# Seven-block left products in a fourth gated step, and layernorms moved between ScalarE and VectorE

## The chip, the core and the metric

The kernel runs on one core of a Trainium2 chip. The engines named here are TensorE (PE, with its weight loads as PEld), VectorE (DVE), ScalarE (ACT), GpSimd (POOL) and SyncE (SP), which issues nearly all transfers. The metric is the device time of one execution in microseconds. The kernel before took 1408.14 us, the median of 3 runs from 1408.05 to 1408.65.

## The reference

The input x holds 64 graphs of 256 nodes with 128 features, in float32, and one adjacency matrix adj (256 x 256) is shared by all. Four graph layers follow each other, each wrapped as x = layernorm(x + layer(x)):

- layer 0: an attention layer with its own way of pairing nodes, a softmax, and a second weight for the node itself
- layer 1: attention with leaky ReLU scores, a softmax over the neighbours, the weighted sum, and an ELU
- layer 2: five gated steps. In each, m = adj @ h; then r, z = sigmoid of (m times a weight + h times a weight), hv = tanh(m times a weight + (r * h) times a weight), and h = (1 - z) * h + z * hv
- layer 3: x times a weight plus adj @ x, adj^2 @ x and adj^3 @ x times weights

The layernorm subtracts the mean over the features and divides by the standard deviation.

## The kernel before

**Units and lanes.** Two graphs make a unit, so there are 32 units, numbered 0 to 31. A unit's data is a tile of 128 partitions by 512 columns: two graphs times two chunks of 128 nodes, times 128 features. Ten lanes (`LANES`) of buffers let ten units be under way at once. Lane k works on units k, k + 10 and so on.

**The planner sets the order.** The kernel doesn't issue instructions as its loops run. `add` records each as a task with an engine, a planned duration, and the cells it reads and writes. `Plan.run` then goes through planned time. Whenever an engine is free it takes the ready task with the smallest key, and the order in which tasks are taken is the order of the program on each engine. The key (`first`) is the unit's number times `PERIOD` plus the task's due time. The due time grows along the unit's own chain of dependences, by the planned duration and a latency, times `PACE` (2.9), or times `PACE_GATED` (1.56) in layer 2. On the chip each engine executes its list in that fixed order, and a late operand holds up everything behind it on that engine. A product can only be planned when one of the 8 PSUM banks is free.

**The left product m = adj @ h in layer 2.** `layer2` has two ways to make it, chosen by `fast = step in FAST and far(u, step - 1)`.

- The plain way, `left` (L771): two products of 256 columns for each of the two graphs, four in all, into one bank. Then ACT copies the bank to m (L839).
- The fast way, `left_fast`: DVE forms sums and differences of the four blocks of h (L781, L783, L784). Seven products of 128 columns (L788) go into two banks x and y. ACT copies the first (L800), and DVE combines the rest into m (L815, L818, L820, L821). The combined blocks of adj lie in `adjTf`.

`far(u, step)` says whether the unit's h is turned by a DVE transpose and transfers through DRAM (the tile `hb`), rather than on PE. Units 0 and 1 start with that from step 2 (`FIRST_FAR`), and unit 31 stops it at step 1 (`LAST_FAR`). With `FAST = (2, 3, 4)` there are 91 fast steps and 69 plain ones.

After m is there, the products of 512 columns with the gate weights follow (L843): h and m for r, then, once ACT has the tanh for r and DVE has r * h, m for hv and z, and r * h with u5. The activations are L854, L862 and L871, and DVE's updates L857, L869, L873 and L875. The new h is transposed on DVE (L883, L896) and sent through `hb`.

**The layernorm.** `layernorm` takes statistics on DVE (L566, L568). POOL raises the variance to the power -1/2 (L571). The four pieces of 128 features are then normalised either on ACT (L584, which needs one more DVE instruction, L575, for the shift) or on DVE (L588, L592):

```
by_act = u >= TIGHT and plan.layer in NORM
```

With `TIGHT = 4` and `NORM = (0, 1, 2, 3)` ACT does it in all four layers from unit 4 on.

**The end.** The last three units (29 to 31) write their output in two transfers, one per chunk of nodes (L955), each after the two normalisations of its chunk. All others use a single one (L951).

Of the kernel before, what the change touches and what calls it, by code (L numbers as in the profile page):

```python
# [18 lines left out]
LEAD = 10  # L19
BANKS = 8  # L20
BL = 32
FAST = (2, 3, 4)
NORM = (0, 1, 2, 3)
SCALES = True
TIGHT = 4
FIRST_FAR = {0: 2, 1: 2}
# [1 line left out]
PERIOD = 43e3  # L28
TAIL = 0.3
LATE = 6  # L30
PACE = 2.9
PACE_GATED = 1.56
HOLD = 80
DIRECT_ROWS = 3
# [28 lines left out]
class Plan:  # L63
# [17 lines left out]
    def add(self, eng, ns, fn, reads=(), writes=(), after=(), wait=0, group=None, dma=False):  # L81
        t = Task(eng, ns, fn, self.unit, wait, dma or eng == "sp")
        for c in reads:
            t.deps.update(c.writers)
            c.readers.append(t)
        for c in writes:
            if c.bank and not c.writers:
                t.takes.append(c)
            if group is None or c.group is not group:
                c.waits = {w for o in (c, *c.over) for w in (*o.writers, *o.readers)} - {t}  # L90
                c.writers, c.readers, c.group = [], [], group
            t.deps.update(c.waits)
            if c.bank and c.writers:

                t.deps.add(c.writers[0])
            c.writers.append(t)
        t.deps.update(after)
        t.deps.discard(t)
        for c in {id(c): c for c in (*reads, *writes) if c.bank}.values():
            c.users += 1  # L100
            t.banks.append(c)
        t.step = self.step = self.step + 1
        t.layer = self.layer
        t.rank = self.rank
        self.tasks.append(t)
        return t
# [4 lines left out]
    def run(self, spawn, units, key):  # L111
# [22 lines left out]
        def start(lane):  # L134
            mine = [u for u in queue if u % LANES == lane]
            if mine:
# [5 lines left out]
                for t in self.tasks[seen:]:  # L142
                    t.due = max([d.due + (PACE_GATED if t.layer == 2 else PACE) * (d.ns + (
                        d.wait + self.LATENCY["sp" if d.dma else d.eng] if d.dma or d.eng != t.eng else self.OWN[t.eng]))
# [52 lines left out]
def kernel(  # L197
# [30 lines left out]
    NC = N // P  # L228
    UB = 2
    NU = B // UB  # L230
# [18 lines left out]
    def bank():  # L249
        return Cell(bank=True)  # L250
# [166 lines left out]
    for t, wT, n in ((wx0, woT, C0), (ws0, wselfT, D + 2)):  # L417
        ps = bank()
# [85 lines left out]
    def far(u, step):  # L504


        return step >= FIRST_FAR.get(u, -1) and step < LAST_FAR.get(NU - 1 - u, STEPS + 1)
# [8 lines left out]
    def turned(u, L, step):  # L516

        t = L["xT0"]  # L520
        if not far(u, step):
            feature_major(X[u], lambda g: X[u].ap[:, g // NC, g % NC, :], t)
            return t
        v = L["v"]
        add(DVE, 1050, lambda: nc.vector.transpose(  # L525
            v.ap.rearrange("p (a g i) -> p g a i", g=G, i=BL),
            X[u].ap.rearrange("p b c (j a) -> p (b c) a j", j=BL)), (X[u],), (v,))
        add("sp", 560, lambda: nc.sync.dma_start(L["hb"].ap, v.ap), (v,), (L["hb"],))
        parts = object()
        for q in range(P // BL):  # L530
            add("sp", 640, lambda q=q: nc.sync.dma_start(
                t.ap.rearrange("p (g q i) -> p g q i", g=G, i=BL)[:, :, q],
                L["hb"].ap[q * BL : (q + 1) * BL].rearrange("j (a g i) -> (j a) g i", g=G, i=BL)),
                (L["hb"],), (t,), group=parts)
        return t
# [20 lines left out]
                ps.ap[:, g * P : (g + 1) * P], view()[:, g : g + 1].to_broadcast([P, P]), ident.ap), (src, ident), (ps,))  # L556
        return ps, lambda: ps.ap.rearrange("q (b c p) -> q b c p", b=UB, c=NC)

    def layernorm(u, L, pairs, swap=False, centred=False):

        st, ve, rstd = L["st"], L["ve"], L["rstd"]
        sts, xs = object(), object()
        for k, (c, view) in enumerate(pairs):
            add(DVE, 330, lambda k=k, view=view: nc.vector.bn_stats(st.ap[:, k, :], view().rearrange("p j d -> p d j")),  # L566
                (c,), (st,), group=sts)
        add(DVE, 150, lambda: nc.vector.tensor_scalar(  # L568
            ve.ap.rearrange("p (k j) -> p k j", k=2), st.ap.rearrange("p k (j s) -> p k j s", j=2)[:, :, :, 2], 1.0 / D, EPS,
            op0=ALU.mult, op1=ALU.add), (st,), (ve,))  # L570
        add(POOL, 1050, lambda: nc.gpsimd.tensor_tensor(rstd.ap, ve.ap, nhalf.ap, op=ALU.pow), (ve, nhalf), (rstd,))  # L571
        by_act = u >= TIGHT and plan.layer in NORM

        if by_act and not centred:
            add(DVE, 120, lambda: nc.vector.scalar_tensor_tensor(  # L575
                ve.ap.rearrange("p (k j) -> p k j", k=2), st.ap.rearrange("p k (j s) -> p k j s", j=2)[:, :, :, 1], -1.0,
                rstd.ap.rearrange("p (k j) -> p k j", k=2), op0=ALU.mult, op1=ALU.mult), (st, rstd), (ve,))
        for k, (c, view) in enumerate(pairs):
            for j in range(2):
                b, ch = (j, k) if swap else (k, j)  # L580
                at = slice(2 * k + j, 2 * k + j + 1)
                shift, col = (ones, slice(0, 1)) if centred else (ve, at)
                if by_act:
                    add(ACT, 400, lambda j=j, b=b, ch=ch, view=view, at=at, shift=shift, col=col: nc.scalar.activation(  # L584
                        X[u].ap[:, b, ch, :], view()[:, j, :], AF.Identity, bias=shift.ap[:, col], scale=rstd.ap[:, at]),
                        (c, shift, rstd), (X[u],), group=xs)
                elif centred:
                    add(DVE, 260, lambda j=j, b=b, ch=ch, view=view, at=at: nc.vector.tensor_scalar(  # L588
                        X[u].ap[:, b, ch, :], view()[:, j, :], rstd.ap[:, at], 1.0, op0=ALU.mult, op1=ALU.add),
                        (c, rstd), (X[u],), group=xs)  # L590
                else:
                    add(DVE, 260, lambda k=k, j=j, b=b, ch=ch, view=view, at=at: nc.vector.tensor_scalar(  # L592
                        X[u].ap[:, b, ch, :], view()[:, j, :], st.ap[:, k, 3 * j + 1 : 3 * j + 2], rstd.ap[:, at],
                        op0=ALU.subtract, op1=ALU.mult), (c, st, rstd), (X[u],), group=xs)
# [172 lines left out]
    def left(ps, src, b, lhs=None, mat=adjT):  # L767

        lhs = lhs or (lambda b, mc: src.ap[:, b, mc, :])
        for mc in range(NC):  # L770
            add(PE, mm_ns(N), lambda b=b, mc=mc: nc.tensor.matmul(  # L771
                ps.ap[:, b * N : (b + 1) * N], lhs(b, mc), mat.ap[:, mc, :],
                start=(mc == 0), stop=(mc == NC - 1)), (src, mat), (ps,))
# [49 lines left out]
    def layer2(u, L):  # L823
        h, ht = turned(u, L, -1), X[u]
        for step in range(STEPS):
            m, at = L["m"], len(plan.tasks)
            fast = step in FAST and far(u, step - 1)
            ps_m = None if fast else bank()
# [94 lines left out]
    def layer3(u, L):  # L923
        xT = turned(u, L, STEPS)
        ps_a, aT, s = bank(), L["m"], L["z"]
        for b in range(UB):
            left(ps_a, X[u], b)
        add(ACT, 500, lambda: nc.scalar.copy(aT.ap, ps_a.ap), (ps_a,), (aT,))
        tail = list(ps_a.writers)

        ps = [bank() for _ in range(NC)]

        def view(c):
            return ps[c].ap.rearrange("p (k b d) -> p k b d", k=2, b=UB)

        for k, src in enumerate((xT, aT)):
            for c in range(NC):
                for b in range(UB):
                    add(PE, mm_ns(N), lambda k=k, src=src, c=c, b=b: nc.tensor.matmul(  # L939
                        view(c)[:, :, b, :], bn(src.ap)[:, b, c * P : (c + 1) * P], w3.ap[:, k],  # L940
                        start=(k == 0 and b == 0), stop=(k == 1), skip_group_check=True), (src, w3), (ps[c],), tail)
        for c in range(NC):
            add(ACT, 300, lambda c=c: nc.scalar.copy(s.ap[:, c * N : (c + 1) * N], ps[c].ap[:, N : 2 * N]), (ps[c],), (s,), group=ps)
        for c in range(NC):
            for mc in range(NC):
                add(PE, mm_ns(N), lambda c=c, mc=mc: nc.tensor.matmul(  # L946
                    ps[c].ap[:, 0:N], a2T.ap[:, mc, c * P : (c + 1) * P], s.ap[:, mc * N : (mc + 1) * N],
                    start=False, stop=(mc == NC - 1), skip_group_check=True), (a2T, s), (ps[c],))
        layernorm(u, L, [(ps[c], lambda c=c: view(c)[:, 0]) for c in range(NC)], swap=True)
        if u < NU - 3:  # L950
            add("sp", 450, lambda: nc.sync.dma_start(out_u[u], X[u].ap), (X[u],), ())  # L951
            return

        for c, done in enumerate((plan.tasks[-4:-2], plan.tasks[-2:])):
            add("sp", 450, lambda c=c: nc.sync.dma_start(out_u[u][:, :, c], X[u].ap[:, :, c]), (), (), done)  # L955
# [50 lines left out]
```

The softmax here doesn't subtract the row's maximum and nothing guards it: scores larger than these inputs give would overflow.

## Time and profile before

| | before |
|---|---|
| median of the runs | 1408.14 us |
| the profiled execution | 1408.72 us |
| its span, first to last instruction | 1406.5 us |
| PE busy | 1396.0 us (99%) |
| DVE busy | 1135.0 us (81%) |
| ACT busy | 939.2 us (67%) |
| POOL busy | 142.4 us (10%) |
| granted PE clock | 0.997 |

A busy time is the time in which at least one instruction of the engine ran. PE's instructions are pipelined and their ends are modelled, so its busy share says less than what it waited for and how far apart its instructions start. A float32 product shows as two instructions. In a group of instructions the columns are the number of them, busy time and mean ns of one, then the idle time of the engine just before them and what ended it. An engine's idle time only matters where it holds up the work that ends last.

### The profile page before, as it was taken

How to read it: one execution, taken by the hardware profiler on the slowest of the kernel's cores; microseconds unless marked ns; L12 is line 12 of the kernel's file. 1: busy time of each engine (PE TensorE's matmuls, PEld its weight loads, DVE VectorE, ACT ScalarE, POOL GpSimd, SP SyncE). 2: the span in 40 equal slices, each digit the busy share in tenths (PEclk: the TensorE clock that was granted, in tenths of full speed). 3: DMA queues.
4: the chain of work that ended last, by engine and by line, in shares of the span. 5: the costliest groups of instructions: out<-in, count | busy, mean ns of one | idle time of the engine just before them, and what ended most of it. 6: DMA issues, size and time to landing. Idle time of an engine off the chain costs nothing.

```text
span 1406.5 us, 20482 instructions
## 1 busy us (share of the span) xinstructions
PE 1396.0 (99%) x6163; PEld 961.8 (68%) x6163; DVE 1135.0 (81%) x2746; ACT 939.2 (67%) x2125; POOL 142.4 (10%) x134
## 2 busy tenths in 40 slices
PE   8999999999999999999999999999999999999998
PEld 8866666676666676676666677676666666666776
DVE  7988888879878788878788788888768888988642
ACT  5797647547766677757677778887766555566454
POOL 0110001001011001011000111021000000101011
PEclk9999999999999999999999999999999999999999
DMA  4213545454554445555445554545554443455411
GB/s 118 61 48 85 120 95 116 100 118 100 132 117 109 97 100 120 121 118 116 99 99 121 126 114 102 114 111 116 116 120 93 107 110 82 116 119 116 110 49 50
DMA packets 533246, 146.96 MB, mean 104 GB/s; under 512 B 460688, under 2 KB 498320, under 8 KB 533136
## 3 DMA queue, kind: packets, MB, share of 16 engines
q1 hardware_dynamic: 532336, 145.13, 46.6%
q8 instruction: 50, 0.82, 0.2%
q14 instruction: 60, 0.49, 0.1%
q10 hardware_dynamic: 800, 0.52, 0.1%
HBM read 81.10 MB, written 64.46 MB: 103 GB/s over the span
## 4 chain that ended last, share of the span: by engine, by line
PE 98%; DVE 1%; ACT 1%; DMA 0%; issue 0%; POOL 0%; SPq 0%; POOLq 0%; ACTq 0%; DVEq 0%
PE ps L843 48%; PE ps L771 12%; PE ps L788 10%; PE ps L939 8%; PE ps L695 4%; PE ps L725 4%; PE ps L946 4%; PE ps L690 2%; PE ps L619 2%; PE ps L738 2%; PE ps L344 0%; DMA m<-row 0%; PE ps L512 0%; PE ps L908 0%; ACT e L714 0%; PE ps L555 0%
## 5 line engine op out<-in xcount | busy, mean ns | idle before, releaser
L843 PE MATMUL ps<-m,gT 128*128 128x512 f32 x960 | 462.4, 593 | 0.4 <-DVE m L821 0.3
L571 POOL TENSOR_TENSOR rstd<-ve,nhalf 128x4 f32<-128x4 f32 x128 | 141.7, 1108 | 1258.9 <-DVE ve L568 1127.3
L843 PEld LDWEIGHTS ps<-m,gT 128*128 128x128 f32 x960 | 173.0, 190 | 124.9 <-issue 102.3
L862 ACT ACTIVATE e<-ps,bias 128x512 f32<-128x512 f32 x160 | 109.9, 688 | 119.4 <-PE ps L843 116.9
L854 ACT ACTIVATE e<-ps,bias 128x512 f32<-128x512 f32 x160 | 109.9, 688 | 84.8 <-PE ps L843 83.7
L843 PE MATMUL ps<-e,u5T 128*128 128x512 f32 x320 | 163.3, 592 | 0.0
L871 ACT ACTIVATE p<-ps,bias 128x512 f32<-128x512 f32 x160 | 109.7, 686 | 41.0 <-PE ps L843 38.5
L771 PE MATMUL ps<-adjT,x 128*128 128x256 f32 x512 | 135.1, 379 | 0.0
L873 DVE SCALAR_TENSOR_TENSOR p<-e,p 128x512 f32<-128x512 f32 x160 | 109.2, 683 | 23.7 <-ACT p L871 22.9
L788 PEld LDWEIGHTS ps<-adjTf,ht 128*128 128x128 f32 x546 | 88.0, 191 | 47.6 <-issue 38.4
L771 PEld LDWEIGHTS ps<-adjT,x 128*128 128x128 f32 x512 | 93.2, 190 | 35.2 <-issue 25.6
L788 PEld LDWEIGHTS ps<-adjTf,e 128*128 128x128 f32 x728 | 95.3, 192 | 15.0 <-issue 12.4
L788 PE MATMUL ps<-adjTf,e 128*128 128x128 f32 x728 | 102.9, 275 | 0.0
L843 PEld LDWEIGHTS ps<-e,u5T 128*128 128x128 f32 x320 | 59.8, 190 | 58.8 <-issue 45.0
L843 PE MATMUL ps<-xT,gT 128*128 128x512 f32 x192 | 97.8, 593 | 0.0
L788 PE MATMUL ps<-adjTf,ht 128*128 128x128 f32 x546 | 91.9, 274 | 0.0
L839 ACT COPY m<-ps 128x512 f32<-128x512 f32 x69 | 40.2, 583 | 70.6 <-PE ps L771 69.7
L857 DVE SCALAR_TENSOR_TENSOR e<-e,xT 128x512 f32<-128x512 f32 x96 | 65.7, 684 | 22.8 <-ACT e L854 22.1
L714 ACT ACTIVATE e<-m,esd 128x256 f32<-128x256 f32 x116 | 83.1, 763 | 0.9 <-DMA m<-row 0.9
L525 DVE STREAM_TRANSPOSE p<-x 128x512 f32<-128x512 f32 x61 | 67.1, 1100 | 15.1 <-ACT x L584 14.7
L695 PEld LDWEIGHTS ps<-ht,p 128*128 128x128 f32 x512 | 66.5, 190 | 12.1 <-issue 11.0
L566 DVE BATCH_NORM_STATS2 st<-ps 128x6 f32<-128x256 f32 x128 | 50.9, 421 | 25.2 <-PE ps L946 19.6
(174 smaller groups left out, 2640.4 us busy)
## 6 DMA issues: line engine op xcount, KB each, us to landing
hb<-p SPq DMA_DIRECT2D x182, 256.0 KB, 2.4
ht<-hb SPq DMA_DIRECT2D x484, 64.0 KB, 2.6
xT<-hb SPq DMA_DIRECT2D x244, 64.0 KB, 2.7
m<-row SPq DMA_DIRECT2D x58, 256.0 KB, 4.0
hb<-p SPq DMA_DIRECT2D x124, 64.0 KB, 1.8
ht<-hb SPq DMA_DIRECT2D x31, 256.0 KB, 3.2
out_dram<-x SPq DMA_DIRECT2D x29, 256.0 KB, 2.5
m<-in_x_dram SPq DMA_DIRECT2D x96, 64.0 KB, 2.7
```

Source lines behind the costliest of these rows:

```text
L525: add(DVE, 1050, lambda: nc.vector.transpose(v.ap.rearrange("p (a g i) -> p g a i", g=G, i=BL), X[u].ap.rearrange("p b c (j a) -> p (b c) ...
L571: add(POOL, 1050, lambda: nc.gpsimd.tensor_tensor(rstd.ap, ve.ap, nhalf.ap, op=ALU.pow), (ve, nhalf), (rstd,))
L695: add(PE, mm_ns(D + 2), lambda b=b, ic=ic, kc=kc, yv=yv: nc.tensor.matmul(yv()[:, ic, :], p.ap[:, b * NC + kc, ic * P : (ic + 1) * P], h.a ...
L714: add(ACT, 600, lambda g=g, b=b: nc.scalar.activation(e.ap[:, g, :].rearrange("p (c n) -> p c n", c=NC), ev()[:, b], AF.Prelu, bias=esd.ap ...
L771: add(PE, mm_ns(N), lambda b=b, mc=mc: nc.tensor.matmul(ps.ap[:, b * N : (b + 1) * N], lhs(b, mc), mat.ap[:, mc, :], start=(mc == 0), stop ...
L788: add(PE, mm_ns(P) + 4, lambda: nc.tensor.matmul(ps.ap[:, at * P : (at + 1) * P], lhs(), mat.ap[:, k, c * P : (c + 1) * P], start=True, st ...
L843: add(PE, mm_ns(T), lambda: nc.tensor.matmul(ps.ap, w(), rhs.ap, start=start, stop=stop, skip_group_check=True), (c, rhs), (ps,), after)
L854: add(ACT, 600, lambda ps_g=ps_g, up=up: nc.scalar.activation(r.ap, ps_g.ap, AF.Tanh, bias=bias2.ap[:, 1:2], scale=0.5 / up), (ps_g, bias2 ...
L862: add(ACT, 600, lambda ps_g=ps_g, up=up: nc.scalar.activation(z.ap, ps_g.ap, AF.Tanh, bias=bias2.ap[:, 0:1], scale=0.5 / up), (ps_g, bias2 ...
L871: add(ACT, 600, lambda ps_v=ps_v, up=up: nc.scalar.activation(v.ap, ps_v.ap, AF.Tanh, bias=bias2.ap[:, 2:3], scale=1 / up), (ps_v, bias2), ...
L873: add(DVE, 600, lambda: nc.vector.scalar_tensor_tensor(v.ap, z.ap, 1.0, v.ap, op0=ALU.add, op1=ALU.mult), (v, z), (v,))
L939: add(PE, mm_ns(N), lambda k=k, src=src, c=c, b=b: nc.tensor.matmul(view(c)[:, :, b, :], bn(src.ap)[:, b, c * P : (c + 1) * P], w3.ap[:, k ...
```

## The change

- `FAST` gains step 1, so step 1 of every unit that is `far` by then is made the fast way.
- `NORM` loses layer 1, so its four normalisations are on DVE in all units.
- `layernorm` gets the argument `last`. It is set in layer 3 for units 29 to 31, and there the first chunk is normalised on DVE and the second on ACT.
- `PACE` goes from 2.9 to 2.8, which changes the due times outside layer 2.

```diff
--- before.py
+++ after.py
@@ -19,8 +19,8 @@
 LEAD = 10
 BANKS = 8
 BL = 32
-FAST = (2, 3, 4)
-NORM = (0, 1, 2, 3)
+FAST = (1, 2, 3, 4)
+NORM = (0, 2, 3)
 SCALES = True
 TIGHT = 4
 FIRST_FAR = {0: 2, 1: 2}
@@ -28,7 +28,7 @@
 PERIOD = 43e3
 TAIL = 0.3
 LATE = 6
-PACE = 2.9
+PACE = 2.8
 PACE_GATED = 1.56
 HOLD = 80
 DIRECT_ROWS = 3
@@ -556,7 +556,7 @@
                 ps.ap[:, g * P : (g + 1) * P], view()[:, g : g + 1].to_broadcast([P, P]), ident.ap), (src, ident), (ps,))
         return ps, lambda: ps.ap.rearrange("q (b c p) -> q b c p", b=UB, c=NC)
 
-    def layernorm(u, L, pairs, swap=False, centred=False):
+    def layernorm(u, L, pairs, swap=False, centred=False, last=False):
 
 
 
@@ -576,11 +576,13 @@
                 ve.ap.rearrange("p (k j) -> p k j", k=2), st.ap.rearrange("p k (j s) -> p k j s", j=2)[:, :, :, 1], -1.0,
                 rstd.ap.rearrange("p (k j) -> p k j", k=2), op0=ALU.mult, op1=ALU.mult), (st, rstd), (ve,))
         for k, (c, view) in enumerate(pairs):
+
+            act = by_act and (k or not last)
             for j in range(2):
                 b, ch = (j, k) if swap else (k, j)
                 at = slice(2 * k + j, 2 * k + j + 1)
                 shift, col = (ones, slice(0, 1)) if centred else (ve, at)
-                if by_act:
+                if act:
                     add(ACT, 400, lambda j=j, b=b, ch=ch, view=view, at=at, shift=shift, col=col: nc.scalar.activation(
                         X[u].ap[:, b, ch, :], view()[:, j, :], AF.Identity, bias=shift.ap[:, col], scale=rstd.ap[:, at]),
                         (c, shift, rstd), (X[u],), group=xs)
@@ -946,7 +948,7 @@
                 add(PE, mm_ns(N), lambda c=c, mc=mc: nc.tensor.matmul(
                     ps[c].ap[:, 0:N], a2T.ap[:, mc, c * P : (c + 1) * P], s.ap[:, mc * N : (mc + 1) * N],
                     start=False, stop=(mc == NC - 1), skip_group_check=True), (a2T, s), (ps[c],))
-        layernorm(u, L, [(ps[c], lambda c=c: view(c)[:, 0]) for c in range(NC)], swap=True)
+        layernorm(u, L, [(ps[c], lambda c=c: view(c)[:, 0]) for c in range(NC)], swap=True, last=u >= NU - 3)
         if u < NU - 3:
             add("sp", 450, lambda: nc.sync.dma_start(out_u[u], X[u].ap), (X[u],), ())
             return
```

The lines after the inserted ones move by 2 in the changed kernel, so L788 is L790 there.

## The prediction

> **What bounds the kernel now.** I read the page's busy times first, then the chain that ended last, then what TensorE (PE) itself waited for, and only then the groups of instructions that the change touches. The page gives the span, the busy time of each engine and the chain by engine:
>
> ```profile
> span 1406.5 us, 20482 instructions
> PE 1396.0 (99%) x6163; PEld 961.8 (68%) x6163; DVE 1135.0 (81%) x2746; ACT 939.2 (67%) x2125; POOL 142.4 (10%) x134
> PE 98%; DVE 1%; ACT 1%; DMA 0%; issue 0%; POOL 0%; SPq 0%; POOLq 0%; ACTq 0%; DVEq 0%
> ```
>
> A modelled busy share of 99% alone would not settle it, but the chain is 98% PE, and the waits of PE (who was waited for, us in total, times, longest) are these three and no more:
>
> ```profile
> PE ps L725 <- DVE p L718: 2.3, 1, 2.3
> PE ps L344 <- POOL ident masks.py:199: 1.4, 1, 1.4
> PE ps L843 <- DVE m L821: 0.3, 1, 0.3
> ```
>
> The first two lie in the first 30 us. From there to about 1398 us PE is fed without a gap, so the time is PE's work plus a start and a tail. Less PE work shortens the kernel by just that amount, as long as VectorE (DVE) still keeps up. The table by stretches says how near DVE is to its own limit (start:end, length, then busy us of PE, PEld, DVE, ACT, POOL). The second row is a usual stretch and the first is the densest after the start-up:
>
> ```profile
> 315.00:350.00 35.00, 35.00 (x154) 22.83 (x153) 33.40 (x84) 26.35 (x62) 4.21 (x4) 1.00 0.45 101
> 595.00:630.00 35.00, 35.00 (x155) 24.48 (x154) 28.73 (x69) 19.83 (x46) 4.43 (x4) 1.00 0.45 99
> ```
>
> Even at 33.40 of 35 us PE did not wait. The prices come from the chain in order of time (start, us) for PE, and from the groups for the others:
>
> ```profile
> 608.16 0.89 PE ps L788 x8
> 610.35 1.73 PE ps L771 x8
> ...
> L781 DVE TENSOR_TENSOR e<-ht 128x256 f32<-128x256 f32 x91 | 37.6, 413 | 0.2 <-DMA ht<-hb 0.2
> L783 DVE TENSOR_TENSOR e<-e,ht 128x128 f32<-128x128 f32 x91 | 25.7, 283 | 0.6
> L784 DVE TENSOR_TENSOR e<-e,ht 128x128 f32<-128x128 f32 x91 | 25.9, 284 | 0.8
> L815 DVE TENSOR_TENSOR m<-ps,e 128x256 f32<-128x256 f32 x91 | 38.2, 420 | 30.6 <-PE ps L788 29.5 <-ACT e L714 0.2
> L839 ACT COPY m<-ps 128x512 f32<-128x512 f32 x69 | 40.2, 583 | 70.6 <-PE ps L771 69.7 <-DVE st L566 0.6 <-ACT e L714 0.2
> L584 ACT ACTIVATE x<-ht,ve,rstd 128x128 f32<-128x128 f32 x112 | 48.9, 485 | 20.4 <-DVE ve L575 20.4
> L592 DVE TENSOR_SCALAR x<-ht,st,rstd 128x128 f32<-128x128 f32 x16 | 4.6, 336 | 0.0
> ```
>
> Each float32 product is recorded as two instructions, so four 256-column products (x8) take 1.73 us and four 128-column ones 0.89 us.
>
> **What the Trainium skill says.** "TensorE: Matmul & The Clock Gate", section Back-to-back issue gap, gives N / 2.4 + 2.5 ns for a warm isolated matmul: 55.8 ns at 128 columns, 109 ns at 256. The trace has four times these per product (0.223 and 0.432 us), so it agrees in ratio: seven small products (28 x 55.8 = 1.56 us) are cheaper than four large ones (16 x 109 = 1.75 us). "VectorE: DVE Perf Modes", section The perf-mode tier table, says that a float32 tensor_scalar runs twice as fast as a tensor_tensor, but not from PSUM. Here L592 takes 336 ns from SBUF and 401 ns from PSUM. "ScalarE: Activation LUTs", section What ACT_TABLE_LOAD costs, prices an activation at 186 ns + 0.833 ns per element plus about 93 ns for each pointer operand. With two of them at 128 elements that is an estimate of 479 ns, against 485 measured.
>
> **The change part by part.** *Step 1 joins the fast steps.* A fast step needs its input by way of the transfer through hb, which units 2 to 31 have at step 1. Units 0 and 1 start that later. So 30 steps change, and fast steps go from 91 to 121. Each loses four L771 products, 4 x 0.4325 = 1.73 us, and gains seven L788 products. At 0.2225 each (0.89 / 4) these are 1.56; where the trace shows eight instructions in 0.90 us they are 1.575. The gain per step is 0.155 to 0.17 us, I take 0.163, and 30 steps give **4.9 us** of PE work (4.65 to 5.2).
>
> DVE gets seven instructions per step: 413 + 283 + 284 + 420 + 413 + 281 + 411 = 2505 ns, or 75.2 us for 30 steps. ACT loses the 583 ns copy L839 and gains the 266 ns copy L800, so 9.5 us less. I cost the DVE work at nothing, since PE's other work hides it. Without cover, a step's product on m would start later by 420 + 413 + 281 + 411 less the copy's 583 = 0.94 us. The cover can be read from the order in which the program's instructions stand on PE. Between the last block of a fast step and the first product that reads its m, the kernel before has at least 2.15 us of other PE work (median 3.9, seven steps at or under 2.2). The changed one has at least 2.19 (median 3.9, and the next shortest 2.6). The four combining instructions need about 1.5 us plus hand-offs, and with that cover 91 steps waited 0.3 us in all. A new step also holds two PSUM banks where it held one. No PE wait of today is for a bank, so that is 0 too.
>
> *Layer 1's normalisation goes to DVE.* Units 4 to 31 are concerned: 28 x 4 = 112 activations of 485 ns leave ACT (54.3 us), 112 tensor_scalars of 336 ns come to DVE (37.6 us), and 28 L575 of 153 ns leave it (4.3 us). Nothing of it is on PE. The unit's own path gets shorter.
>
> The sum for DVE is 1135.0 + 75.2 + 37.6 - 4.3 + 2.4 (the last units, below) = 1246 us of about 1401, or 89%. That is an upper end, because durations overlap: consecutive 512-column operations last 0.69 us and start 0.60 apart. ACT falls to about 873 us. Spread evenly, DVE gets 2.8 us per 35 us. The usual 28.7 becomes 31.5, and the densest 33.4 would become 36.2.
>
> *The last units.* Chunk 0 of the last three units goes to DVE while ACT does chunk 1. Today the last four activations run from 1402.20 to 1403.70, and the two output transfers are issued at 1403.04 and 1403.74. With two on each engine both chunks are ready at about 1402.95. The two issues of 0.37 us each then follow each other on SP, so the second one comes near 1403.4, and I take **0.35 us** (0 to 0.7). Also, today unit 30 ends PE's order behind one covering product (0.43 us) for a copy that needs 0.38 us and two hand-offs: the last eight instructions span 2.19 us where they span 1.89 elsewhere. In the changed order unit 31 is last, behind two covering products, which returns **0.3 us**.
>
> *PACE 2.9 to 2.8* issues nothing. It shifts due times in the planner. PE's order is the same up to the first new fast step (past 100 us), and the transfers are as many as before. I cost it at 0, with rearrangements of up to 1 us either way.
>
> Sum: 4.9 + 0.35 + 0.3 = 5.55, less 0.1 for a chance wait like today's, is 5.45 us. The profiled execution took 1408.72 us (span 1406.5 and 2.2 around it), which becomes 1403.3. The median of the runs is 0.58 lower, so **1402.7**.
>
> **The rivals.** *DVE bounds in its densest stretches.* For it: 33.40 + 2.8 exceeds 35 by 1.2, and 32.41 (945 to 980) by 0.2. Against it: the durations overlap and the planner rearranges. It would cost 1.4 us and give 1404.1.
>
> *The gain is swallowed*, because the new order puts small gaps before PE by bank or transfer waits. At 0.1 us per new step that is 3 us, leaving about 1406. Nothing in today's waits speaks for it.
>
> *Slower:* the product on m waits in each new step, since DVE is crowded and its combining instructions stand behind the new normalisations (4 x 0.34 us). Uncovered, 30 x 0.94 = 28 us, so 1431. It turns the result to slower from (5.45 + 2.8) / 30 = 0.28 us per new step on. Against it: the cover of at least 2.19 us just counted.
>
> *A little better:* no wait at all and the upper end of the PE price, about 1402.2.
>
> **How the numbers follow.** 0.2% of the time, 2.8 us, is about what a measurement of this kernel can tell from no change. Chances: the forecast (1402.2 to 1403.4) 0.63, a little better 0.07, DVE-bound stretches 0.12, swallowed 0.09, slower 0.09. The range 1401.6 to 1405.8 holds the first three, 0.82. Faster means below 1405.3: 0.82. Within 0.2%: 0.09. Slower: 0.09.
>
> **What would show it.** L788's line should count 7 x 121 products (1694 instructions) and L771's 284 (568), at the same spacing. PE's waits should stay below 1 us past the start, DVE should be busy 86 to 89%, ACT about 62%, and the outputs of the last unit issued 0.4 us apart. Waits of L843 for L821 or for DVE normalisations, or a stretch with PE under 34.5 of 35, would prove me wrong.

## The result, and the profile after

The changed kernel takes 1402.72 us (median of 4 runs, 1402.29 to 1402.90) against 1408.10 (4 runs, 1406.73 to 1408.65). The ratio is 0.9963, with a 95% interval of 0.9946 to 0.9980. So it is faster by 0.37%, 5.4 us by the medians, where 5.45 us and 1402.7 us were forecast. The profiled execution took 1402.88 us, 5.84 us less than the one before. Executions of one kernel fall in two groups about 1.8 us apart, with and without a spell at half the granted clock near 30 us, and kernels had unequal shares of them, so the parts are compared below by a stretch of the profiles that begins after that spell.

The page of the changed kernel (span, busy times, chain by engine):

```profile
span 1401.1 us, 21133 instructions
PE 1391.3 (99%) x6343; PEld 963.8 (69%) x6343; DVE 1210.8 (86%) x3046; ACT 884.5 (63%) x2007; POOL 140.7 (10%) x134
PE 99%; DVE 0%; ACT 0%; POOLq 0%; issue 0%; POOL 0%; ACTq 0%; DVEq 0%
```

Its waits of PE (who was waited for, us in total, times, longest):

```profile
PE ps L727 <- DVE p L720: 2.3, 1, 2.3
PE ps L344 <- POOL ident masks.py:199: 1.4, 1, 1.4
```

The picture is that of before with less work on PE. The chain is 99% PE, the two waits of the first 30 us are still there, and even the single 0.3 us wait for the fast step's m is gone. DVE went from 81 to 86% and ACT from 67 to 63%. The groups that the change touches (line numbers are 2 higher now):

```profile
L790 PE MATMUL ps<-adjTf,e 128*128 128x128 f32 x968 | 136.6, 275 | 0.0
L790 PE MATMUL ps<-adjTf,ht 128*128 128x128 f32 x726 | 122.2, 274 | 0.0
L773 PE MATMUL ps<-adjT,x 128*128 128x256 f32 x512 | 132.5, 379 | 0.0
L817 DVE TENSOR_TENSOR m<-ps,e 128x256 f32<-128x256 f32 x121 | 50.6, 418 | 32.4 <-PE ps L790 31.9
L841 ACT COPY m<-ps 128x512 f32<-128x512 f32 x39 | 22.8, 584 | 39.0 <-PE ps L773 38.9
L594 DVE TENSOR_SCALAR x<-ht,st,rstd 128x128 f32<-128x128 f32 x128 | 37.6, 338 | 0.1
```

There are 121 fast steps (968 + 726 = 1694 instructions, 14 each), 39 copies of m are left on ACT, and 112 of layer 1's normalisations have joined the 16 that DVE had.

How close to full DVE runs is seen in the table by stretches of the changed kernel (length, then busy us of PE, PEld, DVE, ACT, POOL, then PE's granted clock, the DMA share and GB/s):

```profile
285.00:290.00 5.00, 5.00 (x26) 3.77 (x25) 5.00 (x14) 1.68 (x3) 0.00 (x0) 1.00 0.88 231
290.00:295.00 5.00, 5.00 (x25) 3.09 (x24) 5.00 (x14) 3.54 (x8) 0.97 (x1) 1.00 0.81 184
295.00:300.00 5.00, 5.00 (x29) 4.18 (x28) 5.00 (x14) 0.59 (x2) 0.41 (x1) 1.00 0.69 158
```

For 15 us DVE has not a moment's rest, and PE is fed all the same. A full DVE needn't hold up PE. When it does is what the experiments turn on.

**Where the 5.4 us came from.** The clearest ruler is from the start of the first fast block to the end of the last product, since PE's order is the same up to that block. Before it is from 101.61 to 1400.08 us (1298.47), after from 102.05 to 1395.00 (1292.95): 5.52 us less. Of these, 0.3 us are the wait that vanished, and 0.3 the hole in front of the very last products. That leaves 4.9 us of PE work. From PE's end to the end of the span it is 6.42 us before and 6.10 after, so the tail gives 0.3 us. The start takes 0.44 us back (102.05 instead of 101.61). And the time outside the span falls from 2.2 to 1.8 us (1408.72 - 1406.5 and 1402.88 - 1401.1), which the forecast took as unchanged. All this sums to the 5.84 us between the profiled executions. The 1.8 us are usual in the runs that have PACE 2.8 or layer 1's layernorm on DVE, and 2.2 us in those with neither. What it is isn't known.

The end in the order of time, first of the kernel before, then of the changed one (start, us; in brackets the idle time before it and what ended it):

```profile
1397.89 2.19 PE L946 MATMUL ps<-e,a2T 128*128 128x256 f32 x8
1402.20 1.50 ACT L584 ACTIVATE x<-ps,ve,rstd 128x128 f32<-128x128 f32 x4 [0.92 <-DVE ve L575]
1403.04 1.07 SPq L955 DMA_DIRECT2D out_dram<-x  x2
```

```profile
1392.25 2.75 PE L948 MATMUL ps<-e,a2T 128*128 128x256 f32 x12
1397.04 0.72 DVE L594 TENSOR_SCALAR x<-ps,st,rstd 128x128 f32<-128x128 f32 x2
1397.22 0.81 ACT L586 ACTIVATE x<-ps,ve,rstd 128x128 f32<-128x128 f32 x2 [0.51 <-DVE ve L575]
1397.79 0.88 SPq L957 DMA_DIRECT2D out_dram<-x  x2
```

Two activations take 0.81 us where four took 1.50, and DVE's two normalisations run beside them. The last two issues (0.37 us each) start 0.51 us apart instead of 0.70.

### The profile page after: what moved, and what is told of

Its sections match the earlier page's. It is cut to its first block, busy times and chain, and to the rows that moved or that the text cites. A ratio compares the mean times of both kernels' runs of the same rounds, so it can differ in the third digit from the quotient of the medians.

```text
span 1401.1 us, 21133 instructions
## 1 busy us (share of the span) xinstructions
PE 1391.3 (99%) x6343; PEld 963.8 (69%) x6343; DVE 1210.8 (86%) x3046; ACT 884.5 (63%) x2007; POOL 140.7 (10%) x134
## 4 chain that ended last, share of the span: by engine, by line
PE 99%; DVE 0%; ACT 0%; POOLq 0%; issue 0%; POOL 0%; ACTq 0%; DVEq 0%
PE ps L845 49%; PE ps L790 13%; PE ps L773 9%; PE ps L941 8%; PE ps L697 4%; PE ps L727 4%; PE ps L948 4%; PE ps L621 2%; PE ps L692 2%; PE ps L740 2%; PE ps L344 0%; PE ps L512 0%; PE ps L910 0%; PE ps L555 0%; PE ps L646 0%; PE ps L487 0%
## 5 line engine op out<-in xcount | busy, mean ns | idle before, releaser
L845 PE MATMUL ps<-m,gT 128*128 128x512 f32 x960 | 466.1, 592 | 0.1
L845 PEld LDWEIGHTS ps<-m,gT 128*128 128x128 f32 x960 | 172.1, 190 | 121.9 <-issue 97.6
L790 PEld LDWEIGHTS ps<-adjTf,ht 128*128 128x128 f32 x726 | 116.9, 191 | 67.6 <-issue 58.5
L845 PE MATMUL ps<-e,u5T 128*128 128x512 f32 x320 | 163.3, 592 | 0.0
L790 PEld LDWEIGHTS ps<-adjTf,e 128*128 128x128 f32 x968 | 125.9, 192 | 17.9 <-issue 14.7
L790 PE MATMUL ps<-adjTf,e 128*128 128x128 f32 x968 | 136.6, 275 | 0.0
L790 PE MATMUL ps<-adjTf,ht 128*128 128x128 f32 x726 | 122.2, 274 | 0.0
L773 PEld LDWEIGHTS ps<-adjT,x 128*128 128x128 f32 x512 | 93.2, 190 | 38.7 <-issue 29.5
L845 PEld LDWEIGHTS ps<-e,u5T 128*128 128x128 f32 x320 | 60.1, 190 | 64.6 <-issue 48.3
L845 PE MATMUL ps<-xT,gT 128*128 128x512 f32 x192 | 96.8, 593 | 0.0
L817 DVE TENSOR_TENSOR m<-ps,e 128x256 f32<-128x256 f32 x121 | 50.6, 418 | 32.4 <-PE ps L790 31.9
L697 PE MATMUL ps<-ht,p 128*128 128x130 f32 x512 | 69.7, 275 | 0.0
```

Of the source, the lines that this page charges most:

```text
L697: add(PE, mm_ns(D + 2), lambda b=b, ic=ic, kc=kc, yv=yv: nc.tensor.matmul(yv()[:, ic, :], p.ap[:, b * NC + kc, ic * P : (ic + 1) * P], h.a ...
L773: add(PE, mm_ns(N), lambda b=b, mc=mc: nc.tensor.matmul(ps.ap[:, b * N : (b + 1) * N], lhs(b, mc), mat.ap[:, mc, :], start=(mc == 0), stop ...
L790: add(PE, mm_ns(P) + 4, lambda: nc.tensor.matmul(ps.ap[:, at * P : (at + 1) * P], lhs(), mat.ap[:, k, c * P : (c + 1) * P], start=True, st ...
L845: add(PE, mm_ns(T), lambda: nc.tensor.matmul(ps.ap, w(), rhs.ap, start=start, stop=stop, skip_group_check=True), (c, rhs), (ps,), after)
```

## The experiments

Theory: the gain is the PE work of the 30 steps that became fast, and all else is hidden or neutral. Rivals: another part carries the gain or makes it possible; DVE is at its limit and takes a part back; the order in which the planner puts the work decides. The first four runs do one part each, on the kernel before.

**FAST alone.**

```diff
-FAST = (2, 3, 4)
+FAST = (1, 2, 3, 4)
```

> Only FAST = (1, 2, 3, 4) added to the kernel before; layernorms, PACE and the last units as before. If the gain is PE work (30 steps x 0.163 us), this alone gives 4.9 us, so about 1403.2 us beside 1408.1, with PE waits past the start under 1 us. If the rest of the change carries a good part of it (room that the other parts make), this gives clearly less than 4 us.

Measured: 1402.52 us, ratio 0.9968 (0.9955 to 0.9980). From the first fast block to the last product it is 99.81 to 1393.52, so 1293.71 us, 4.8 less than before, where the whole change gives 5.5. The list of waits has nothing past the start, with DVE at 1187.7 us. The hole of 0.3 us ahead of the last products is still there, and the starts of PE's instructions show two more of that size, at 832 and 1378 us. So this part alone gives most of the gain, though the medians make it look like all of it.

**Layer 1's layernorm alone.**

```diff
-NORM = (0, 1, 2, 3)
+NORM = (0, 2, 3)
```

> Only layer 1's layernorm on DVE. PE issues the same instructions, so the PE-work theory says 0 (within 0.5 us of 1408.1), with DVE about 33 us busier and ACT about 54 us less busy. If the shorter path of the unit or the free ACT mattered, it would gain 1 us or more; if DVE were near its limit, it would lose 1 us or more.

Measured: 1408.70 us, ratio 1.0003 (0.9995 to 1.0012), with DVE 23.7 us busier and ACT 38.7 us less busy. PE waits once past 200 us, 0.5 us, for a combining instruction on DVE. Neither the freed ACT nor the busier DVE makes a difference here that can be told.

**The last units alone.** The argument `last` in `layernorm` as in the change, on the kernel before.

```diff
-        layernorm(u, L, [(ps[c], lambda c=c: view(c)[:, 0]) for c in range(NC)], swap=True)
+        layernorm(u, L, [(ps[c], lambda c=c: view(c)[:, 0]) for c in range(NC)], swap=True, last=u >= NU - 3)
```

> Only the last three units' first chunk normalised on DVE beside the second on ACT. The forecast's tail step says 0.35 us less, from the two output transfers of the last unit issued about 0.4 us apart instead of 0.7; the other 0.3 us (PE's end, order of units 30 and 31) should come only if the planner's order changes at the end as it did in the whole change. If the last transfer's landing hides it, 0.

Measured: 1407.95 us, ratio 1.0000 (0.9992 to 1.0008). No gain, and the trace shows that it is absent and not only too small to see. From PE's end (1397.45 + 2.19 = 1399.64) to the end of the span (1406.1) it is 6.46 us, not less than before. The timeline of this kernel:

```profile
1397.45 2.19 PE L948 MATMUL ps<-e,a2T 128*128 128x256 f32 x8
1399.22 0.72 DVE L594 TENSOR_SCALAR x<-ps,st,rstd 128x128 f32<-128x128 f32 x2
1399.86 0.75 DVE L566 BATCH_NORM_STATS2 st<-ps 128x6 f32<-128x256 f32 x2
1402.01 0.72 DVE L594 TENSOR_SCALAR x<-ps,st,rstd 128x128 f32<-128x128 f32 x2
```

The normalisation of unit 31, moved to DVE, now stands in front of the statistics of unit 30, which ends PE's order here. They begin 0.2 us after PE's end. In the kernel before and in the changed one they begin 0.3 us before it, as soon as their first bank is done. What the split wins after the statistics is lost ahead of them. In the changed kernel unit 31 ends PE's order, with more room to unit 30, and so the gain of 0.3 us stays. The run with both NORM and PACE undone (below) has the split too, ends with unit 30, and has no gain in the tail either (6.47 us).

**PACE alone.**

```diff
-PACE = 2.9
+PACE = 2.8
```

> Only PACE 2.9 to 2.8: the same instructions in another order. PE-work theory: within 0.5 us of 1408.1. If the order is what gives the gain, 2 us or more less; if only the combination with the other parts needs it, 0 here too, or somewhat slower.

Measured: 1407.09 us, ratio 0.9996 (0.9988 to 1.0004). No difference that can be told. PE's one wait of the kernel before is still there, with 0.2 us.

**The dose: no fast step at all**, in the changed kernel.

```diff
-FAST = (1, 2, 3, 4)
+FAST = ()
```

> The changed kernel with FAST empty: all 160 left products the plain way. If a seven-block product is worth 0.163 us of PE and nothing else counts, 121 of them missing cost 19.7 us: about 1422.4 us. DVE falls by 120 to 300 us. If the fast way also paid in other ways (or cost hidden waits), the difference per step would not be 0.155 to 0.17 us.

Measured: 1422.40 us, ratio to the kernel before 1.0100 (1.0086 to 1.0113). By the ruler (102.01, where the first left product now begins the plain way, to 1414.67) it is 1312.66 us, 19.71 more than the changed kernel, so 0.163 us for each of 121 steps. DVE falls to 994.9 us. The price per step is the forecast's own.

**All layernorms on DVE**, in the changed kernel.

```diff
-NORM = (0, 2, 3)
+NORM = ()
```

> The changed kernel with NORM empty: all four layernorms of all units on DVE, PE's instructions unchanged. DVE rises from 1211 us busy to between 1285 and 1320 (92 to 94%). If DVE has reserve up to there, within 1 us of 1402.7. If DVE bounds in its dense stretches (33.6 of 35 us now, 2 to 3 us more each), PE waits for DVE appear and cost 3 us or more.

Measured: 1412.77 us, ratio 1.0035 (1.0023 to 1.0047): 10 us more than the changed kernel, with the same PE instructions. The profiled execution took 1416.39 us, the longest of six. In it DVE is at 1285.8 us (91%). The waits of PE, the two longest:

```profile
PE ps L845 <- DVE m L823: 5.9, 4, 1.8
PE ps L727 <- DVE p L720: 2.6, 2, 2.3
```

The first of these spots in order of time (start us, us):

```profile
134.16 0.83 PE L790 MATMUL ps<-adjTf,e 128*128 128x128 f32 x6
136.84 1.72 PE L845 MATMUL ps<-m,gT 128*128 128x512 f32 x2 [1.84 <-DVE m L823]
```

This is the slower rival's mechanism: the product on m waits for the last combining instruction of a fast step. The product on m comes directly after the blocks' products in the order, with nothing in between. By their spacing it could have started at 134.83, and it starts 2.0 us later. It doesn't happen all over the kernel: four waits make up 5.9 us.

**More fast steps.** First step 0 in all units, then layer 3's left product as well. A second set of combined blocks in natural node order (`adjTn`, made from `adjT` as `adjTf` is from `adjTp`) is set up at the start.

```diff
-            fast = step in FAST and far(u, step - 1)
+            fast = step in FAST and far(u, step - 1) or not step
...
-                left_fast(ht, lambda g: gd(ht.ap)[:, g], adjTf, L["r"], L["z"], m)
+                rows = gd(ht.ap) if step else gd(ht.ap.rearrange("p b c d -> p (b c d)"))
+                left_fast(ht, lambda g, rows=rows: rows[:, g], adjTf if step else adjTn, L["r"], L["z"], m)
```

For layer 3 (in the second run only):

```diff
...
-        for b in range(UB):
-            left(ps_a, X[u], b)
-        add(ACT, 500, lambda: nc.scalar.copy(aT.ap, ps_a.ap), (ps_a,), (aT,))
+        rows = gd(X[u].ap.rearrange("p b c d -> p (b c d)"))
+        left_fast(X[u], lambda g: rows[:, g], adjTn, L["r"], L["z"], aT)
...
```

> The changed kernel with step 0 fast too, in all 32 units, from a second set of combined adjacency blocks in natural node order. PE-work theory: 32 x 0.163 = 5.2 us less than the changed kernel, about 1397.5 us; DVE about 1270 to 1290 us busy (91 to 92%). If DVE begins to bound, the gain is under 3 us and PE shows waits for DVE.

> As the one with step 0, and layer 3's left product the fast way as well: 64 seven-block products more than the changed kernel. PE-work theory: 10.4 us less than 1402.7, about 1392.3 us. DVE would be at 1320 to 1370 us, 95 to 98%: the theory that DVE becomes the bound says that this gains clearly less than 10 us, or loses, with PE waiting for DVE by several us.

Measured: 1417.18 us (ratio 1.0062, 1.0050 to 1.0075) and 1428.01 us (ratio 1.0144, 1.0130 to 1.0157), where PE work alone would have given 1397.5 and 1392.3. DVE is at 1264.0 and 1313.9 us (89 and 92%). PE waits in many places for DVE and a few times for ACT. In the first one PE is busy for 96.35 of the 100 us from 100 to 200, in the second for 94.98. So the method's saving on PE doesn't go on for ever, but the reason could be the start (the extra set-up, units 0 to 9) or DVE's load.

**Step 0 from unit 10 on**, with layer 1's layernorm on ACT (first run, with the edit of NORM) and on DVE (second run, without it), both from the run with step 0 fast:

```diff
-            fast = step in FAST and far(u, step - 1) or not step
+            fast = step in FAST and far(u, step - 1) or not step and u >= LANES
...
-NORM = (0, 2, 3)
+NORM = (0, 1, 2, 3)
```

> The changed kernel with step 0 fast too for units 10 to 31 (22 steps), and layer 1's layernorm back on ACT. PE work says 22 x 0.163 = 3.6 us less than the changed kernel, about 1399.1 us. DVE would be at about 1235 us (88%), between the changed kernel's 86% and the 91% at which all norms on DVE cost 10 us. If DVE's load is what decides, most of the gain comes and this beats both kernels; if the loss of the earlier trial with step 0 came from its start (units 0 to 9), the same; if fast steps at step 0 are bad in themselves, it is slower than 1402.7.

> As the one before, but with layer 1's layernorm on DVE as in the changed kernel: DVE at about 1255 us (90%). PE instructions the same in number. DVE-load theory: clearly slower than the one with that layernorm on ACT, by 3 us or more, with PE waiting for DVE; if only the start-up mattered, both are near 1399.

Measured: 1411.03 us (ratio 1.0021, 1.0013 to 1.0030) with DVE at 1224.7 us, and 1410.64 us (1.0021, 1.0013 to 1.0028) with DVE at 1247.2 us. Both lose, by the same amount, though one has 22.5 us less on DVE. From 100 to 200 us PE is now fed (100.00 and 99.98 of 100), so a part of the earlier loss lay at the start. The expectation that DVE's total decides has failed, and so has the one that only the start matters. From 60 us on, the starts of PE's instructions lie 10.3 and 10.9 us further apart in all than their usual spacing gives (within 0.4 us of it before, after and with FAST alone). So the loss against PE work is gaps on PE, most of it at 15 and 13 places. In the first kernel the most is waited for ACT there: 1.5, 1.1 and 0.8 us for L868, beside 1.0 for m on DVE. The products that wait for L868 don't read what it writes. It reads a bank (e<-ps) that they write next, so these are waits for a PSUM bank, which the prediction counted as 0 since it saw none in the kernel before. How much of the loss the extra banks of the fast steps cause isn't settled.

**The layernorm part undone**, in the changed kernel.

```diff
-NORM = (0, 2, 3)
+NORM = (0, 1, 2, 3)
```

> The changed kernel with only the layer 1 part undone (layernorm on ACT). DVE falls from 1211 to about 1188 us. PE-work theory with DVE below its limit in both: 1402.7 within 0.5 us. If the changed kernel already pays for DVE at 86%, this is 1 us or more faster; if the DVE layernorm helped by its shorter path, slower.

Measured: 1407.98 us, ratio 1.0002 (0.9994 to 1.0011). With less on DVE than the changed kernel (1187.5 us), the whole gain is gone. The order of time on PE shows where most of it went:

```profile
292.57 0.61 PE L790 MATMUL ps<-adjTf,ht 128*128 128x128 f32 x4
293.02 1.02 PE L845 MATMUL ps<-xT,gT 128*128 128x512 f32 x2
296.26 2.08 PE L845 MATMUL ps<-m,gT 128*128 128x512 f32 x2 [2.22 <-DVE m L823]
```

The same time on DVE:

```profile
293.75 0.41 DVE L820 TENSOR_TENSOR m<-ps,m 128x256 f32<-128x256 f32 x1
294.08 0.69 DVE L885 STREAM_TRANSPOSE p<-p 128x512 f32<-128x512 f32 x1
294.70 0.24 DVE L822 TENSOR_TENSOR m<-ps,m 128x128 f32<-128x128 f32 x1
294.88 0.65 DVE L662 TENSOR_REDUCE nm<-e 128x4 f32<-128x512 f32 x1
295.47 0.40 DVE L783 TENSOR_TENSOR e<-ht 128x256 f32<-128x256 f32 x1
295.80 0.40 DVE L823 TENSOR_TENSOR m<-ps,m 128x256 f32<-128x256 f32 x1
```

And the table by stretches around it (start:end, then columns as above):

```profile
290.00:295.00 5.00, 4.04 (x23) 2.58 (x21) 5.00 (x11) 1.29 (x4) 0.00 (x0) 1.00 0.67 135
295.00:300.00 5.00, 3.74 (x13) 2.71 (x14) 4.09 (x12) 2.63 (x10) 1.85 (x1) 0.66 0.57 119
```

DVE instructions of other steps and layers (L885, L662 and L783) stand between this step's combining ones, and only 1.3 us of PE work (two products on L790, four records, and the one of L845 on xT) between its last block and the product on m. PE waits 2.2 us, and then its granted clock falls to 0.66 in the next 5 us: a pair of 512-column instructions takes 2.08 us instead of 1.02. That second loss is about 1.7 us (5 x 0.34). Two more waits, 0.9 and 0.7 us for ACT, come later in the run. Together that is 5.5 us, of the 6.5 us by which the ruler (101.39 to 1400.87, so 1299.48 us) is longer than in the changed kernel.

In this order 1.3 us is the shortest cover of all fast steps, and the next is 2.16. With all layernorms on DVE three steps have 0.0, 0.2 and 1.5 us, and their products on m start 1.9 to 2.0 us late. FAST alone, the changed kernel and the last run below have at least 2.15, and no wait for m is listed.

But the cover alone doesn't tell which step waits. The kernel before has its one wait of 0.3 us where the cover is 6.0 us, and none at its shortest, 2.15. There the blocks end near 233.1 us:

```profile
232.24 1.06 PE L788 MATMUL ps<-adjTf,e 128*128 128x128 f32 x8
239.61 1.55 PE L843 MATMUL ps<-m,gT 128*128 128x512 f32 x3 [0.29 <-DVE m L821]
```

On DVE the combining instructions are spread over 4 us:

```profile
235.54 0.42 DVE L815 TENSOR_TENSOR m<-ps,e 128x256 f32<-128x256 f32 x1
236.93 0.29 DVE L820 TENSOR_TENSOR m<-ps,m 128x128 f32<-128x128 f32 x1
237.39 1.23 DVE L718 TENSOR_TENSOR p<-e,mask 128x1024 f32<-128x1024 f32 x1 [0.17 <-ACT e L717]
238.53 0.69 DVE L869 SCALAR_TENSOR_TENSOR p<-e,xT 128x512 f32<-128x512 f32 x1
239.14 0.42 DVE L821 TENSOR_TENSOR m<-ps,m 128x256 f32<-128x256 f32 x1
```

The traces of all kernels here have 19 fast gated steps with less than 2 us of cover. The product on m starts 1.5 to 2.4 us later than the usual spacing in eight of them, 0.7 us late in one, and no more than 0.2 us late in ten (one with only 0.9 us of cover). Of the other 1542, all with 2.15 us or more, none is later than 0.7 us. So a short cover is where the long waits are, but whether one comes depends also on what stands between the combining instructions on DVE.

**Both NORM and PACE undone**, in the changed kernel, which leaves FAST and the last units.

```diff
-NORM = (0, 2, 3)
+NORM = (0, 1, 2, 3)
...
-PACE = 2.8
+PACE = 2.9
```

> The changed kernel with both NORM and PACE as before: layer 1's layernorm on ACT, PACE 2.9. Together with the run that undid NORM alone (1407.98), it tells whether layer 1's place or the resulting order costs the 5 us. In this order the cover between the last block of a fast step and the product on m is at least 2.15 us (1.3 us in the run that undid NORM alone, at the spot of its 2.2 us wait). If the order decides: about 1402, as with FAST alone, perhaps 0.3 us less by the last units; if the layernorm on ACT costs in itself once PACE or the last units are changed, 1405 or more.

Measured: 1403.87 us, ratio 0.9965 (0.9951 to 0.9979), no wait of PE past the start. Layer 1's layernorm on ACT is harmless in this order, and costs all the gain in that with PACE 2.8. So the place of the layernorm in itself is not what matters. The fourth combination, FAST with PACE 2.9 and the layernorm on DVE, was not run. By the ruler this run is as FAST alone (1293.71 us), 0.8 us behind the changed kernel. No other run beats the changed kernel by more than the intervals.

## Why the prediction was right, and where it was lucky

- **PE work of 30 steps, 4.9 us:** right. The ruler gives 4.9 once the two small holes are taken off, FAST alone gives 4.8 of the ruler's 5.5 us, and 121 steps cost 19.7 us, 0.163 each, to be without.
- **DVE's extra work at nothing:** right for this order, where 15 us of a full DVE pass without a wait of PE. DVE came to 1210.8 us, below the upper end of 1246, as said, because durations overlap. The rival that DVE bounds in its densest stretches added up busy time per 35 us. That sum doesn't tell here: the run with layer 1's layernorm back on ACT had less DVE work and lost 5 us, and the two with step 0 from unit 10 on lost the same with 22.5 us between them.
- **Cover of at least 2.19 us:** right in what came of it, no wait for m, but with some luck. Over 2 us of cover kept every wait under 0.7 us in these runs. Yet the 0.3 us wait that the prediction set beside its shortest covers stood at 6.0 us of cover, and a wait of 0.5 us in the run with all layernorms on DVE at 2.4. The prediction counted PE's side only, and left out what stands between the combining instructions in DVE's order. The slower rival's price of 0.94 us per uncovered step was too low for the same reason, since it took them one behind the other. With others in between, single spots cost up to 2.4 us, and some of these gaps were followed by a spell at a low clock.
- **PACE and layer 1's layernorm at 0:** right for the sum and each alone, but the reason given was too simple. They don't add: from the changed kernel, undoing NORM alone brings 5.3 us back, and undoing both 1.2 us by the medians, within the scatter. "Rearrangements of up to 1 us either way" was the mis-sized term. The runs showed 5 us.
- **The last units, 0.35 us:** 0.3 measured, but not as worked out. The second issue did not queue behind the first on SP: it came 0.51 us later, since ACT's two activations took 0.81 us. And it depends on unit 31 being last on PE; the same edit alone gave nothing. The hole ahead of the last products, 0.3 us, closed as said.
- **The total:** that it is met to 0.1 us is in part luck. Two terms were not in the sum, a start 0.44 us later and 0.44 us less outside the span, and they cancel. The 0.1 us put aside for a chance wait like that of the kernel before was not needed, and that wait's own 0.3 us came as a gain.
- **A factor that isn't seen:** the prediction names a factor of two between tensor_scalar and tensor_tensor. By its own lines 128 columns take 336 ns as TENSOR_SCALAR (L592) and 283 ns as TENSOR_TENSOR (L783). Its price was the measured one, so nothing rests on the factor.

## What to carry to other kernels

When one engine is fed without a gap, price a change by the spacing of its instructions, and look at the hand-overs in the order itself, from both sides: how much work of the fed engine stands between the blocks and the consumer, and what stands between the producer's instructions on the helper engine. The busy share of the helper engine didn't tell here, neither over the span nor over stretches. With an order made by a planner, each parameter can move a hand-over below its cover, so parts that are worth nothing by themselves can still decide whether the gain of another part arrives.

## What was not expected of the hardware

- A gap of 2.4 us on PE (293.88 to 296.26 us, layernorm part undone) was followed by a granted clock of 0.50 from 296.06 to 299.47 us, so that it cost almost twice its length. With all layernorms on DVE, two of three gaps of about 2 us were followed by the same (0.50 from 137.24 to 140.65 and from 154.31 to 157.72 us), and the third, up to 320.1 us, was not. The spell was 3.4 us long each time.
- The same spell is in the start of the profiles of before (30.28 to 33.69 us) and after (31.36 to 34.78), and not in that of FAST alone, where the first fast block starts at 99.8 us instead of 101.6.
